# An edge convolution on a graph: which batches fetch their rows without gathers, and how far gathers and features are asked for ahead

## The chip, the cores and the metric

One core of a Trainium2 chip runs the kernel. The metric is the device time of one execution in microseconds, and the time given for the kernel is the median of its runs.

## The reference

Graph with N = 12500 nodes (160 features each) and 400000 edges sorted by destination. What is computed, with the weights' scalings left out:

```python
h = relu(layernorm(x))
y0 = h[:, :64] @ W_l1_0 * attr            # rows y = (y0, y1) of every node, 160 values
y1 = einsum('nuc,uv->nvc', h[:, 64:].reshape(n, 32, 3), W_l1_1) * attr
w  = silu(edge_attr_16 @ fc_W1) @ fc_W2   # 192 weights for each edge
ys0, ys1 = y0[src], y1[src]               # gather by edge
mid0 = concat([w_a * ys0 * e0, w_d * (ys1 . e1)])
mid1 = concat([(w_b * ys0) x e1, w_c * e0 * ys1])
z0, z1 = segment sums of mid0, mid1 over dst
out = x + C_S * (h0 @ W_sc0, h1 @ W_sc1) * attr + C_X * (z0 @ W_l2_0, z1 @ W_l2_1) * attr
```

Here e0 and e1 are the first and the other three columns of edge_attr_4.

## The kernel before, in words

**Node stage.** 98 tiles of 128 nodes, in steps of two (HN). x is loaded into acc, normalised, transposed, multiplied by wy and written as ys to a table y_d in HBM, from which the edge stage gathers rows. Beside it POOL already fetches rows of x (not y) for XB = 18 batches of edges into xr (`x_fetch`, L378): 72 indirect DMAs, each held back by a map (po, L485) six steps earlier. SP issues the loads of x, the stores of y_d (L497), the weights' loads (L296), the first features (L393), and `row_index` (L267): twelve DMAs that bring the source indices of the row batches into ri. At the end of the stage DVE scales ri to byte offsets (`row_place`, L271).

**Edge stage.** 3125 tiles of 128 edges, four tiles to a batch: NB = 782 batches. For batch b:
- rows of y come into a tile of yg (six buffers) by four indirect DMAs on POOL (`gather`, L603), one for each tile. They are asked for AHEAD batches before their use, two tiles at a time, and a dependency written by hand keeps the fetches behind the sums (L681) of the batch AHEAD places earlier.
- the features of the edges (xe, one block for eight batches) are asked for EARLY batches ahead on SP (`features`, L393).
- PE makes hidden values (L630; px) and weights (`weigh`, L651; pw), DVE multiplies them with the rows (`products`: own L665, sel L667, pr L561 and L565), PE sums by selection matrices into pz (`sums`, L681).
- sorted destinations let a group of four windows share one matrix: a window is 24, 12, 8, 6, 4 and at last 3 tiles, so a group is 24 down to 3 batches long (three from batch 624 on). At a group's end DVE transposes pz into za (L687, L688), PE applies wo (`linear`, L694) and places the result (`add`, L706), and DVE adds it to acc (L717).
- every 24 batches a block of indices and edge values is loaded on SP (`e4_load`, L401 to L405), related to its windows on DVE (`relate`), joined on ACT (`e4_join`), and its drel is stored by SP (L419).

Two kinds of batches need no gather on POOL:
- **x batches**, `x_batch(u)` for u < 18: every 16th batch from 19 on. Their rows of x lie in xr since the node stage. The mean and scale of each source node are looked up by PE with one-hot matrices (`hot`, `hot_turn` L776, `look_up` L788, `pick`), ACT centers the rows (`x_center`), PE transposes (`x_turn`, L803 and L804) and maps them (`x_map`, L816 and L817), and the scale goes into the edge values (`x_scale`, L823).
- **row batches**, `row_batch(i)`: 72 + 64i, twelve of them. SP fetches each of their 512 rows by a DMA of its own (`row_fetch`, L623), in chunks of 16 spread over the 64 batches from 64i on, into xr where an x batch has been, or, for the first, into a tile rg.

**Node pairs** (49; `skip_load` to `skip_add`) add the second product, h by ws, to acc: x is loaded again, centered, transposed (L741, L742), multiplied (L751, L752) and added (L760). They come every nine batches from batch 296 on, behind the last x batch.

The order of the instructions on each engine is the order of the program (a manual schedule); each engine waits where its next instruction's inputs or buffers aren't ready. SP runs through its part of the program ahead of the others.

Of the kernel before, what the change touches and what calls it, by code (L numbers as in the profile page):

```python
# [10 lines left out]
F32 = mybir.dt.float32  # L11
# [8 lines left out]
P = 128  # L20
M0 = 64
M1 = 32
D = M0 + 3 * M1
# [6 lines left out]
GT = 4  # L30
# [6 lines left out]
MW = BLK // WTS[-1]  # L37
GN = 8
HN = 2
AHEAD = 4  # L40
EARLY = 8
SB = 16
LATE = 8
XB = 18
SK = 9
RB = 64
RN = 16
LO = D - P
EPS = 1e-5
# [5 lines left out]
def kernel(  # L55
# [19 lines left out]
    nc = tc.nc  # L75
# [47 lines left out]
    GE = NG - LATE  # L123
# [20 lines left out]

    ygp = ctx.enter_context(tc.tile_pool(name="yg", bufs=6))
    ld = ctx.enter_context(tc.tile_pool(name="ld", bufs=2))
    evp = ctx.enter_context(tc.tile_pool(name="ev", bufs=2))
    rp = ctx.enter_context(tc.tile_pool(name="rel", bufs=2))
    RF = RB + 8
    NR = (NB - 1 - RF) // RB + 1  # L150
    RP = 4
    assert NR - 1 <= XB and RP * NR <= P
    ri = const.tile([RP * NR, P // RP * GT], I32, name="ri")
    rg = const.tile([P, GT, D], F32, name="rg")
    blocks, ev4, lows = {}, {}, {}

    before = ctx.enter_context(ExitStack())
# [105 lines left out]
    def row_index():  # L263
        t = row_batch(0) * GT
        for i in range(NR):
            t = row_batch(i) * GT
            nc.sync.dma_start(ri[RP * i:RP * (i + 1), :].rearrange("q (p k) -> q p k", k=GT),  # L267
                              src[:, t:t + GT].rearrange("(q p) k -> q p k", q=RP))

    def row_place():  # L270
        nc.vector.tensor_scalar(ri, ri, float(D * 4), None, ALU.mult)  # L271
# [86 lines left out]

    def x_batch(u):

        return SB * (u + 1) + 3

    def x_index(us):
        t = x_batch(0) * GT
        every = src[:, t:t + XB * SB * GT].rearrange("p (u r) -> p u r", r=SB * GT)[:, :, 0:GT]
        nc.sync.dma_start(xi[:, us, :], every[:, us, :])

    def x_split():

# [16 lines left out]
    def features(b):  # L386
        blk = b * GT // BT
        if blk not in blocks:

            xe = ld.tile([P, 512], F32, name="xe")  # L390
            v = e16[blk * P:(blk + 1) * P, :].rearrange("(s k f) (h c) -> k s (f h) c", s=4, k=2, h=2)
            for k in range(2):
                nc.sync.dma_start(xe[:, 256 * k:256 * (k + 1)], v[k])  # L393
            blocks[blk] = xe
# [30 lines left out]
    with (  # L425
# [81 lines left out]
        for i, (g, n) in enumerate(groups[:LEAD]):  # L507
            load_x(g, n)
            if i == 1:
                x_index(slice(2, XB))  # L510
                nc.sync.dma_start(a_sb, attr)
        last = len(steps) - 1
        more = list(groups[LEAD:])
# [1 line left out]
        for q in range(len(steps) + 7):  # L515
            if q <= last and steps[q][2] == 0 and more:
                load_x(*more.pop(0))
            for f in range(XB * GT * q // (last + 6), min(XB * GT * (q + 1) // (last + 6), XB * GT)):
                x_fetch(f, mapped.get(q - 6))
            if q == 8:  # L520
                e4_load(0)
            if q == 10:
                row_index()
            for load in loads[2 * q - 24:2 * q - 22] if q >= 12 else []:
                load()
            if q == 24:
                for b in range(min(EARLY, NB)):
                    features(b)
            if q == 16:
                rows_of_windows()  # L530
                lowest(0)
            if q == 18:
                pt = nd_ph.tile([MW, P], F32, name="ph")[:windows_in(0), :]
                turn_low(0, pt)
                most(0, pt)
            if q == 22:
                spread(0, nd_ph.tile([P, MW], F32, name="ph")[:, :windows_in(0)])
            for stage, lag in ((scales, 3), (leave, 7), (out_of_psum, 4), (roots, 2), (turn_rows, 3), (map_rows, 5),
                               (moments, 0), (center, 1)):
                if 0 <= q - lag <= last:  # L540
                    stage(q - lag)
            if q == 2:
                node_weights()
            if q == last + 3:
                nc.vector.tensor_scalar(nm, mv[:, :, 0], -1.0, None, ALU.mult)
                x_split()
                edge_weights()
                relate(rp, 0)
                row_place()
        assert 12 + len(loads) // 2 <= last and x_batch(XB) <= NB  # L550
    before.close()


# [14 lines left out]
    with (  # L568
# [43 lines left out]
        def row_fetch(i, n):  # L612

            b = row_batch(i)
            if n == 0:
                rows[b] = xr[:, i - 1, :, :] if i else rg
            q, o = divmod(n * RN, P // RP * GT)
            _, at_row = nc.values_load_multi_w_load_instructions(
                ri[RP * i + q:RP * i + q + 1, o:o + RN], engines=[mybir.EngineType.SP], min_val=0, max_val=(N - 1) * D * 4,
                skip_runtime_bounds_check_because="places of nodes, as the indices of the other fetches")  # L620
            for m, v in enumerate(at_row):
                e, k = divmod(n * RN + m, GT)
                nc.sync.dma_start(rows[b].bitcast(U8)[e:e + 1, k, :], y_b[ds(v, D * 4)].unsqueeze(0))  # L623
# [200 lines left out]

        NU = (NT + HN - 1) // HN
        skips = {4: skip_center, 5: skip_turn, 7: skip_map, 8: lambda u: skip_load(u + 1) if u + 1 < NU else None}
        SS, MAP = SB * XB + 8, 7
        xs_of = {x_batch(u) for u in range(XB)}
        rows_of = {row_batch(i) for i in range(NR)}
        assert not xs_of & rows_of and RF + RB * (NR - 1) < NB - 1  # L830
        chunks = [(i, n) for i in range(NR) for n in range(P * GT // RN)]

        K, KB = 3, BLK // GT
        waiting = []
# [7 lines left out]
        def extras(b):  # L842

            g = group_of[b]
            k = b - first_of[g]
            q, r = divmod(b, KB)
            u, v = divmod(b, SB)
            su, sv = divmod(b - SS, SK)
            if b % 2 == 0 and b + 4 < NB:
                s = (b + 4) // 2  # L850
                activate(s, hidden(s))
            if g and k == 0:
                linear(g - 1)
            if b == SS - 8:
                skip_load(0)
            skip = skips.get(sv) if 0 <= su < NU else None
            if skip and sv != MAP:
                skip(su)
            if r == KB - 11 and q + 1 < NQ:
                spread(q + 1, p_x.tile([P, MW], F32, name="px")[:, :windows_in(q + 1)])  # L860
            if u < XB:
                if v == 2:
                    hot_turn(u)
                elif v == 7:
                    x_center(u)
                elif v in (9, 10):
                    x_turn(u, HN * (v == 10))
                elif v == 11:
                    x_map(u, 0)
            if v == 1 and 0 < u <= XB:  # L870
                x_map(u - 1, HN)
            if g and k == 1:
                left(lambda: accumulate(g - 1))
                add(g - 1)
            if skip and sv == MAP:
                left(lambda: skip_add(su))
                skip(su)
            if u < XB and v in (3, 6):
                left(None)
                picked = look_up(u, HN * (v == 6))  # L880
                waiting[-1] = lambda: pick(u, HN * (v == 6), *picked)
            if r == KB - 6 and q + 2 == NQ:
                left(None)
                cnt = p_x.tile([1, 1], F32, name="px")
                any_far(cnt)
                waiting[-1] = lambda: far_flag(cnt)
            if r == KB - 13 and q + 1 < NQ:
                left(None)
                low_pt = p_x.tile([MW, P], F32, name="px")[:windows_in(q + 1), :]
                turn_low(q + 1, low_pt)  # L890
                waiting[-1] = lambda: most(q + 1, low_pt)
# [12 lines left out]
        for b in range(NB):  # L904
            g = group_of[b]
            k = b - first_of[g]
            if b + EARLY < NB:
                features(b + EARLY)
            q, r = divmod(b, KB)
            if r == 0:  # L910
                e4_load(q + 1)
            if r == KB - 4:
                e4_join(q + 1)
            u, v = divmod(b, SB)
            su, sv = divmod(b - SS, SK)
            if b + 2 < NB:
                weigh(b + 2)
            if b + 1 < NB:
                products(b + 1)
            while waiting and b + K < NB:  # L920
                waiting.pop(0)()
            if v == SB - 2 and u < XB:
                x_scale(u)
            if v == 11 and u + 1 < XB:
                hot(u + 1)
# [9 lines left out]
            for m, part in ((b + AHEAD - 1, slice(2, GT)), (b + AHEAD, slice(0, 2))):  # L935
                if AHEAD <= m < NB and m not in xs_of and m not in rows_of:
                    gather(m, part)
            while chunks and chunks[0][0] * RB + chunks[0][1] * RB * RN // (P * GT) <= b:
                row_fetch(*chunks.pop(0))
            while waiting and b + K >= NB:  # L940
                waiting.pop(0)()
            extras(b)
        while waiting:
            waiting.pop(0)()
        assert SS + NU * SK <= first_of[GE] + K and NQ > 1
        for h in ([NG - 2] if NG > 1 else []) + [NG - 1]:
            for k, stage in enumerate((linear, add, accumulate)):
                if h == NG - 1 or min(k, 1) > NB - 1 - first_of[NG - 1]:
# [159 lines left out]
```

## Time and profile before

| | |
|---|---|
| median of 3 runs | 3925.41 us (3924.81 to 3928.84) |
| the profiled execution | 3917.68 us |
| its span | 3915.5 us |
| PE busy | 3586.6 us (92%) |
| DVE busy | 2748.4 us (70%) |
| POOL busy | 2917.6 us (75%) |
| ACT busy | 623.6 us (16%) |
| moved by DMA | 329.82 MB, mean 84 GB/s |
| first gather of the edge stage starts | 100.48 us |
| last one starts | 3892.30 us |

How to read it: a row of the groups gives line, engine, operation, output and inputs with their shapes, a count, then busy time in us and the mean in ns of one, and behind the second bar the idle time of the engine just before these instructions with what ended it ("issue": nothing that the profile shows was waited for). A row of the waits gives who waited for whom: us in total, times, longest. A row of a timeline gives start, duration, and in brackets the idle time before. PEld is the weight load of PE. SPq is the queue of SP; its rows are DMA issues.

### The profile page before, as it was taken

How to read it: one execution, taken by the hardware profiler on the slowest of the kernel's cores; microseconds unless marked ns; L12 is line 12 of the kernel's file. 1: busy time of each engine (PE TensorE's matmuls, PEld its weight loads, DVE VectorE, ACT ScalarE, POOL GpSimd, SP SyncE). 2: the span in 40 equal slices, each digit the busy share in tenths (PEclk: the TensorE clock that was granted, in tenths of full speed). 3: DMA queues.
4: the chain of work that ended last, by engine and by line, in shares of the span. 5: the costliest groups of instructions: out<-in, count | busy, mean ns of one | idle time of the engine just before them, and what ended most of it. 6: DMA issues, size and time to landing. Idle time of an engine off the chain costs nothing.

```text
span 3915.5 us, 66013 instructions
## 1 busy us (share of the span) xinstructions
PE 3586.6 (92%) x17274; PEld 2321.5 (59%) x17274; DVE 2748.4 (70%) x6899; ACT 623.6 (16%) x1863; POOL 2917.6 (75%) x3085
## 2 busy tenths in 40 slices
PE   7898999999999999889999999989899999999988
PEld 7555555555656655555555565555566666666555
DVE  7566666666667666666677677777677777778776
ACT  6111111111111111111111111111111111111111
POOL 6777777777777777777777777777777777777775
PEclk8899999999999999999999999999999999999999
DMA  8333333323333232333333333333333333333324
GB/s 233 78 79 76 78 78 76 77 73 78 77 75 78 74 80 75 83 83 80 80 82 77 84 79 82 80 80 79 82 80 83 80 79 82 83 80 79 79 74 135
DMA packets 262773, 329.82 MB, mean 84 GB/s; under 512 B 78472, under 2 KB 213160, under 8 KB 262392
## 3 DMA queue, kind: packets, MB, share of 16 engines
q0 software_dynamic: 147696, 252.26, 26.2%
q1 hardware_dynamic: 114072, 73.01, 6.7%
q8 instruction: 140, 2.29, 0.2%
q14 instruction: 241, 1.97, 0.2%
q10 hardware_dynamic: 624, 0.27, 0.0%
HBM read 307.70 MB, written 17.61 MB: 83 GB/s over the span
## 4 chain that ended last, share of the span: by engine, by line
PE 42%; DMA 20%; DVE 18%; issue 11%; POOL 8%; DVEq 1%; SPq 0%; ACT 0%; POOLq 0%; ACTq 0%
PE pz L681 22%; DMA yg<-y_d,src_q 19%; POOL yg L603 8%; PE pw L651 8%; DVE pr L565 7%; PE px L630 5%; DVE pr L561 4%; PE px L694 3%; PE px L706 1%; DVE za L687 1%; DVE at L226 1%; DVE za L688 1%; DVE acc L717 1%; DVE own L665 0%; PE po L485 0%
## 5 line engine op out<-in xcount | busy, mean ns | idle before, releaser
L603 POOL DMA_INDIRECT yg<-y_d,src_q x3005 | 2847.2, 947 | 945.9 <-issue 658.2
L681 PE MATMUL pz<-pr,sel 128*128 128x320 f32 x6250 | 1965.7, 459 | 14.8 <-DVE za L688 14.7
L681 PEld LDWEIGHTS pz<-pr,sel 128*128 128x128 f32 x6250 | 1162.6, 196 | 597.9 <-issue 231.1
L561 DVE TENSOR_TENSOR pr<-pw,yg 128x512 f32<-128x512 f32 x752 | 517.9, 689 | 800.4 <-DMA yg<-y_d,src_q 799.2
L651 PE MATMUL pw<-w,hT 64*128 64x192 f32 x6250 | 737.4, 354 | 252.5 <-DVE pr L565 236.1
L651 PEld LDWEIGHTS pw<-w,hT 64*128 64x128 f32 x6250 | 506.1, 189 | 535.4 <-issue 396.8
L565 DVE TENSOR_TENSOR pr<-pw,yg 128x384 f32<-128x384 f32 x1504 | 760.7, 547 | 0.0
L667 DVE TENSOR_TENSOR sel<-own,pw 128x512 f32<-128x512 f32 x782 | 537.0, 687 | 27.0
L630 PE MATMUL px<-xe,w 32*128 32x512 f32 x782 | 437.3, 640 | 8.8 <-DVE acc L717 7.1
L635 ACT ACTIVATE hT<-px 128x512 f32<-128x512 f32 x391 | 233.4, 597 | 1297.1 <-PE px L630 1292.8
L556 ACT ACTIVATE pw<-ev 128x20 f32<-128x20 f32 x782 | 149.3, 191 | 1417.1 <-PE pw L651 1201.8
L687 DVE STREAM_TRANSPOSE za<-pz 128x160 f32<-128x160 f32 x598 | 203.8, 341 | 233.7 <-PE pz L681 232.8
L694 PEld LDWEIGHTS px<-wo,za 128*128 128x128 f32 x1500 | 211.5, 191 | 106.6 <-issue 68.0
L694 PE MATMUL px<-wo,za 128*128 128x160 f32 x1500 | 243.0, 309 | 8.8 <-DVE high L193 4.3
L630 PEld LDWEIGHTS px<-xe,w 32*128 32x128 f32 x782 | 114.2, 183 | 185.0 <-issue 173.3
L688 DVE STREAM_TRANSPOSE za<-pz 32x160 f32<-32x160 f32 x598 | 201.7, 337 | 20.4
L665 DVE TENSOR_TENSOR own<-iota,pw 128x128 f32<-128x128 f32 x782 | 198.4, 254 | 18.3 <-ACT pw L556 14.7
L706 PE MATMUL px<-os,place 128*128 128x160 f32 x600 | 112.0, 309 | 8.3 <-DVE place L698 3.6
L717 DVE SCALAR_TENSOR_TENSOR acc<-px,a_sb,acc 128x160 f32 x300 | 113.8, 379 | 7.5 <-PE px L706 1.5
L706 PEld LDWEIGHTS px<-os,place 128*128 128x128 f32 x600 | 90.7, 190 | 38.5 <-issue 19.7
L378 POOL DMA_INDIRECT xr<-in_x,xi x72 | 69.2, 962 | 29.2 <-PE po L485 13.7
L696 ACT ACTIVATE os<-px 128x160 f32<-128x160 f32 x150 | 45.6, 304 | 229.6 <-PE px L694 228.6
(131 smaller groups left out, 1380.1 us busy)
## 6 DMA issues: line engine op xcount, KB each, us to landing
xr<-y_d SPq DMA_DIRECT2D x5632, 0.6 KB
yg<-y_d,src_q POOLq DMA_INDIRECT x3005
xe<-in_e SPq DMA_DIRECT2D x196, 128.0 KB
rg<-y_d SPq DMA_DIRECT2D x512, 0.6 KB
xs<-in_x SPq DMA_DIRECT2D x48, 160.0 KB
acc<-in_x SPq DMA_DIRECT2D x11, 640.0 KB
y_d<-ys SPq DMA_DIRECT2D x11, 640.0 KB
out<-acc SPq DMA_DIRECT2D x11, 640.0 KB
```

Of the source, the lines that this page charges most:

```text
L561: nc.vector.tensor_mul(pr[:, :n, :].rearrange("p t (x u) -> p t x u", x=2)[:, :, :, 0:M0], wt[:, :n, 0:NW].rearrange("p t (x u) -> p t x u ...
L565: nc.vector.tensor_mul(pr[:, :n, D * x + M0:D * (x + 1)].rearrange("p t (c u) -> p t c u", c=3), wt[:, :n, 96 * x + M0:96 * (x + 1)].unsqu ...
L603: fetch = nc.gpsimd.indirect_dma_start(out=yg[:, slot(t), :], out_offset=None, in_=y_d, in_offset=bass.IndirectOffsetOnAxis(ap=ev4[t // BL ...
L630: nc.tensor.matmul(ph, w1[r, :], xe[r, :], start=True, stop=True)
L635: nc.scalar.activation(hT, ph, AF.Silu, scale=1.0 / math.sqrt(FC_IN))
L651: nc.tensor.matmul(pw[:, k, 0:NW], hT[r, o:o + P], w2[r, :], start=True, stop=True)
L667: nc.vector.tensor_tensor(sel, own[:, :n, :].unsqueeze(2).to_broadcast([P, n, 4, WN]), wt[:, :n, NW:NW + 4].unsqueeze(3).to_broadcast([P, ...
L681: mm = nc.tensor.matmul(pz[:, 0:PC], sel[:, slot(t), :, :], pr[:, slot(t), :], start=o == 0, stop=last)
L687: nc.vector.transpose(zT[g][:, :, at_w], pz[:, D:PC].rearrange("p (k u) -> p k u", k=ZK))
L688: nc.vector.transpose(zT[g][0:32, :, at_w], pz[0:32, 0:D].rearrange("p (k u) -> p k u", k=ZK))
L694: nc.tensor.matmul(po[:m, :], za[:, k, :m], wo[:, k, :], start=k == 0, stop=k == ZK - 1)
L706: nc.tensor.matmul(ps[:, h, :], place[:m, h, :], os[:m, :], start=True, stop=True)
```

## The change

- AHEAD from 4 to 6: gathers are asked for six batches ahead, behind the sums of the batch six earlier; yg keeps its six buffers.
- EARLY from 8 to 16, and xe gets a pool of its own with three buffers instead of two.
- x batches are PER = 43 apart (19, 62, ... 750) instead of 16 (19, 35, ... 291). Behind each one's work (the first 16 batches of a period) three node pairs follow in the same period, nine batches each; the last pair ends at batch 712.
- row batches are 92 + 61i, still twelve; their chunks begin at batch 24 + 61i. All twelve take a place in xr; rg is gone. `row_index` moves from the node stage to batch 0 of the edge stage, `row_place` to batch 2.
- the indices of the last x batch get a DMA of their own (`x_index_last`), since the strided view would reach beyond the array.
- `x_scale` runs 3 batches before its x batch instead of 5.

```diff
-AHEAD = 4
-EARLY = 8
+AHEAD = 6
+EARLY = 16
 SB = 16
+PER = 43
...
-RB = 64
+RB = 61
+RS = 24
...
+    fe = ctx.enter_context(tc.tile_pool(name="fe", bufs=3))
...
-    RF = RB + 8
+    RF = RS + RB + 7
...
-    rg = const.tile([P, GT, D], F32, name="rg")
...
 def x_batch(u):
-        return SB * (u + 1) + 3
+        return PER * u + SB + 3
...
+    def x_index_last():
+        t = x_batch(XB - 1) * GT
+        nc.sync.dma_start(xi[:, XB - 1, :], src[:, t:t + GT])
...
-            xe = ld.tile([P, 512], F32, name="xe")
+            xe = fe.tile([P, 512], F32, name="xe")
...
-                x_index(slice(2, XB))
+                x_index(slice(2, XB - 1))
+                x_index_last()
...
-            if q == 10:
-                row_index()
...
-                row_place()
...
-                rows[b] = xr[:, i - 1, :, :] if i else rg
+                rows[b] = xr[:, i, :, :]
...
-        SS, MAP = SB * XB + 8, 7
+        PAIRS, MAP = (PER - SB) // SK, 7
...
+        def skip_of(b):
+            u, v = divmod(b, PER)
+            if v < SB:
+                return -1, -1
+            return PAIRS * u + (v - SB) // SK, (v - SB) % SK
...
-            u, v = divmod(b, SB)
-            su, sv = divmod(b - SS, SK)
+            u, v = divmod(b, PER)
+            su, sv = skip_of(b)
...
-            if b == SS - 8:
+            if b == SB - 8:
                 skip_load(0)
...
-            if v == 1 and 0 < u <= XB:
-                x_map(u - 1, HN)
+            if v == SB + 1 and u < XB:
+                x_map(u, HN)
...
+            if b == 0:
+                row_index()
...
+            if b == 2:
+                row_place()
-            if v == SB - 2 and u < XB:
+            if v == SB and u < XB:
                 x_scale(u)
...
-            while chunks and chunks[0][0] * RB + chunks[0][1] * RB * RN // (P * GT) <= b:
+            while chunks and RS + chunks[0][0] * RB + chunks[0][1] * RB * RN // (P * GT) <= b:
                 row_fetch(*chunks.pop(0))
```

More of the change, by code (lines that the diff above doesn't have):

```diff
@@ L146 @@
     ld = ctx.enter_context(tc.tile_pool(name="ld", bufs=2))
+    fe = ctx.enter_context(tc.tile_pool(name="fe", bufs=3))
     evp = ctx.enter_context(tc.tile_pool(name="ev", bufs=2))
     rp = ctx.enter_context(tc.tile_pool(name="rel", bufs=2))
-    RF = RB + 8
+    RF = RS + RB + 7
     NR = (NB - 1 - RF) // RB + 1
     RP = 4
-    assert NR - 1 <= XB and RP * NR <= P
+    assert NR <= XB and RP * NR <= P and PER < RB
     ri = const.tile([RP * NR, P // RP * GT], I32, name="ri")
-    rg = const.tile([P, GT, D], F32, name="rg")
     blocks, ev4, lows = {}, {}, {}
@@ L359, in x_batch @@
     def x_batch(u):
-        return SB * (u + 1) + 3
+        return PER * u + SB + 3
     def x_index(us):
         t = x_batch(0) * GT
-        every = src[:, t:t + XB * SB * GT].rearrange("p (u r) -> p u r", r=SB * GT)[:, :, 0:GT]
+        every = src[:, t:t + (XB - 1) * PER * GT].rearrange("p (u r) -> p u r", r=PER * GT)[:, :, 0:GT]
         nc.sync.dma_start(xi[:, us, :], every[:, us, :])
+    def x_index_last():
+        t = x_batch(XB - 1) * GT
+        nc.sync.dma_start(xi[:, XB - 1, :], src[:, t:t + GT])
     def x_split():
@@ L548 @@
                 relate(rp, 0)
-                row_place()
-        assert 12 + len(loads) // 2 <= last and x_batch(XB) <= NB
+        assert 12 + len(loads) // 2 <= last and x_batch(XB - 1) < NB - 1
     before.close()
@@ L913 @@
                 e4_join(q + 1)
-            u, v = divmod(b, SB)
-            su, sv = divmod(b - SS, SK)
+            u, v = divmod(b, PER)
+            su, sv = skip_of(b)
             if b + 2 < NB:
@@ L944 @@
             waiting.pop(0)()
-        assert SS + NU * SK <= first_of[GE] + K and NQ > 1
+        assert max(b for b in range(NB) if 0 <= skip_of(b)[0] < NU) <= first_of[GE] + K and NQ > 1
         for h in ([NG - 2] if NG > 1 else []) + [NG - 1]:
```

## Prediction

> **What bounds the kernel now.** I read the page's busy times first, then the groups, then the waits, then POOL in order of time, then the windows.
>
> ```profile
> PE 3586.6 (92%) x17274; PEld 2321.5 (59%) x17274; DVE 2748.4 (70%) x6899; ACT 623.6 (16%) x1863; POOL 2917.6 (75%) x3085
> L603 POOL DMA_INDIRECT yg<-y_d,src_q x3005 | 2847.2, 947 | 945.9 <-issue 658.2
> ```
>
> By busy time PE is fullest. But the POOL group has 945.9 us of idle time in front of its gathers, and the waits tell what that is:
>
> ```profile
> DVE pr L561 <- DMA yg<-y_d,src_q: 799.2, 483, 5.7
> POOL yg L603 <- issue: 658.2, 2159, 0.4
> POOL yg L603 <- PE pz L681: 93.1, 248, 2.3
> ```
>
> Most of the idle time is 2159 gaps of 658.2 / 2159 = 0.305 us in which nothing was waited for. The gap belongs to the gather, as the timeline of POOL shows (start, duration, and the idle time before in brackets): one start every 1.25 us, whatever released it.
>
> ```profile
> 739.24 0.95 POOL L603 DMA_INDIRECT yg<-y_d,src_q  x1 [0.30 <-issue]
> 740.49 0.94 POOL L603 DMA_INDIRECT yg<-y_d,src_q  x1 [0.30 <-issue]
> 743.79 0.95 POOL L603 DMA_INDIRECT yg<-y_d,src_q  x1 [2.36 <-PE px L198]
> 745.05 0.95 POOL L603 DMA_INDIRECT yg<-y_d,src_q  x1 [0.30 <-issue]
> 746.81 0.94 POOL L603 DMA_INDIRECT yg<-y_d,src_q  x1 [0.82 <-PE pz L681]
> ...
> 3891.05 0.95 POOL L603 DMA_INDIRECT yg<-y_d,src_q  x1 [0.30 <-issue]
> 3892.30 0.95 POOL L603 DMA_INDIRECT yg<-y_d,src_q  x1 [0.30 <-PE pz L681]
> ```
>
> So a gather costs POOL 0.947 + 0.305 = 1.252 us, a batch of four 5.01 us, and all 3005 take 3762 us. The first starts at 100.48 (row below), the last ends at 3893.25: 3793 us. POOL sets the edge stage, and only 945.9 - 3005 x 0.305 = 29.4 us of that stretch are waits that could go. The windows say the same, and where the waits are (stretch, its length, then PE, PEld, DVE, ACT, POOL busy with counts, granted clock):
>
> ```profile
> 100.00:120.00 20.00, 11.69 (x53) 7.27 (x51) 8.48 (x17) 1.55 (x6) 15.12 (x17) 0.78 0.34 87
> 100.00:560.00 460.00, 407.85 (x1883) 253.45 (x1880) 286.56 (x643) 74.73 (x220) 346.88 (x367) 0.96 0.31 78
> 560.00:1020.00 460.00, 428.58 (x2001) 269.46 (x2000) 305.17 (x698) 78.58 (x229) 342.35 (x362) 0.97 0.31 76
> 1020.00:1480.00 460.00, 434.00 (x2077) 276.64 (x2076) 318.67 (x748) 80.20 (x235) 340.10 (x359) 0.98 0.31 76
> 2120.00:3120.00 1000.00, 924.02 (x4435) 597.99 (x4434) 729.12 (x1833) 135.49 (x420) 753.08 (x796) 0.97 0.32 80
> ```
>
> Gathers times 1.252: 460 of 460 us, 453 of 460, 449 of 460, 997 of 1000. The losses sit mainly where x batches are 16 apart: a batch that POOL needn't gather puts it 5 us ahead, it runs into the limit of four batches, and waits for the sums (743.79 and 746.81 are the gathers just behind row batch 136 with x batch 131 before it: 2.06 + 0.52 us over the usual gap).
>
> A rule weighed: the Trainium skill (Perfetto Trace Analysis, Identifying the Most-Contended Engine) says to improve the engine of highest occupancy, but not to judge TensorE by its matmul busy time. By PE's 92% nothing would come of fewer POOL waits, and the time would stay; by the page's measures (weight loads 59%, POOL 75%) POOL is the one, as the gaps above show.
>
> **The change part by part.**
>
> *Number of gathers.* 18 x batches and 12 row batches before and after (the last are 72 + 64i before, 92 + 61i after): still 3005 gathers, 3762 us. This floor doesn't move; the change can earn the 29.4 us and something in the node stage, no more.
>
> *Spread and lead of six.* Skipped batches come 30 in 782 evenly, one in 26, instead of 22 in the first 296 and 8 in the other 486. POOL's average need becomes 5.01 x 752 / 782 = 4.82 us a batch everywhere. PE must need less than that to catch up behind each skipped batch. Its need without extras, in the last part, where a group is only three batches long, from the chain at the end, which is all PE there (eight runs of sums, seven steps):
>
> ```profile
> 3859.69 2.35 PE pz L681 x8
> ...
> 3890.81 2.35 PE pz L681 x8
> ```
>
> 31.12 / 7 = 4.45 us a batch. The extras on PE (busy time of all their instructions):
>
> ```profile
> L752 PE MATMUL px<-ws,sT 128*128 128x96 f32 x196 | 40.5, 288 | 0.0
> L751 PE MATMUL px<-ws,sT 128*128 128x64 f32 x196 | 34.4, 257 | 1.5 <-DVE acc L717 1.5
> L788 PE MATMUL px<-look,sT 128*128 128x196 f32 x144 | 31.6, 342 | 0.0
> L817 PE MATMUL px<-wy,sT 128*128 128x96 f32 x144 | 29.8, 288 | 0.0
> L741 PE MATMUL px<-ident,sh 128*128 128x128 f32 x98 | 25.1, 283 | 4.1 <-ACT hT L635 4.1
> L816 PE MATMUL px<-wy,sT 128*128 128x64 f32 x144 | 24.9, 254 | 0.0
> L742 PE MATMUL px<-ident,sh 128*128 128x128 f32 x98 | 24.1, 273 | 0.0
> L803 PE MATMUL px<-ident,xr 128*128 128x128 f32 x72 | 18.8, 288 | 2.0 <-DVE acc L717 2.0
> L804 PE MATMUL px<-ident,xr 128*128 128x128 f32 x72 | 18.0, 277 | 0.0
> L776 PE MATMUL px<-ident,oh 128*128 128x128 f32 x72 | 11.8, 286 | 0.0
> ```
>
> An x batch: (11.8 + 31.6 + 18.8 + 18.0 + 24.9 + 29.8) / 18 = 7.5 us. A node pair: (25.1 + 24.1 + 34.4 + 40.5) / 49 = 2.5 us. After, 43 batches hold one x batch and three pairs: 15.1 / 43 = 0.35 a batch. So in the worst part PE needs 4.45 + 0.35 = 4.80 against POOL's 4.82: just enough. Earlier, with longer groups, it needs less. Locally, batches 624 to 712 hold the work of two x batches and 6.5 pairs: 88 x 4.45 + 31.4 = 423 us against 84 x 5.01 = 421 for POOL; then 712 to 782 (no pairs, one x batch): 319 against 68 x 5.01 = 341. PE falls behind by what the skipped batches give POOL, some 10 to 13 us, and makes it up before the end. Two batches more of lead are 2 x 4.8 = 9.6 us more room; the stalls that it must take in are about 2.6 us at the largest place shown. Twice (275 and 277, 578 and 580) two skipped batches are two apart: 5 us more, still inside. Remaining stalls: between 0 and 15 us; I take 3, near the 3.4 us that the stretch from 2120 lost with a lead of four. Edge stage: -26.4.
>
> The sixth buffer of yg is free in time: the gather waits for the sums of the batch six back, and the products that read the buffer come before these. So no wait is added that the lead itself doesn't bring.
>
> *Moved row indices (SP, DVE), third feature buffer.* SP in order of time:
>
> ```profile
> 3.25 3.40 SPq L511 DMA_DIRECT2D a_sb<-in_attr  x1
> ...
> 21.69 11.39 SPq L267 DMA_DIRECT2D ri<-in_src  x12
> 33.19 0.41 SPq L497 DMA_DIRECT2D y_d<-ys  x1
> ...
> 57.17 1.20 SPq L393 DMA_DIRECT2D xe<-in_e  x2
> ...
> 97.34 0.48 SPq L401 DMA_DIRECT2D raw<-in_e  x1
> ...
> 100.31 26.01 SPq L623 DMA_DIRECT2D rg<-y_d  x64
> ```
>
> The twelve issues held SP for 11.4 us in the node stage, with a store of y_d behind them. They go behind the last store, to about 98 to 110. There, behind them on SP, are the next block's indices (due at batch 18) and the row fetches, which now begin at batch 24: nothing due. The scaling of ri on DVE (0.28 us, row below) stands behind the products of batch 3, which need gathers that end at 120; ri should be there by 113. Cost 0. In the node stage come two issues of xe (1.2 us) and one more of xi (under the 3.4 us of the nearest row). What the node stage gains goes through POOL, which does 72 fetches there:
>
> ```profile
> POOL xr L378 <- PE po L485: 13.7, 24, 2.2
> 71.81 0.94 POOL L378 DMA_INDIRECT xr<-in_x,xi  x1 [2.22 <-PE po L485]
> 75.94 0.94 POOL L378 DMA_INDIRECT xr<-in_x,xi  x1 [0.68 <-PE po L485]
> 100.48 0.94 POOL L603 DMA_INDIRECT yg<-y_d,src_q  x1 [0.30 <-issue]
> L271 DVE TENSOR_SCALAR ri<-ri 48x128 int32<-48x128 int32 x1 | 0.3, 280 | 0.0
> ```
>
> 13.7 - 24 x 0.305 = 6.4 us of true waits at most; if SP was not the cause, 0, or +2 for the added issues. I take the two late ones, 1.92 + 0.38: -2.3. Row fetches: 26.01 / 64 = 0.406 us an issue, 208 us for 512, in 61 x 4.82 = 294 us instead of 64 x 4.85 = 310; the last is issued by batch 83 of 92, 39 us ahead: 0. Features 16 ahead: no wait for xe is among the large ones, 0 (a late one is bounded by SP's 1.2 us).
>
> *End.* From the last gather to the span's end, 22.3 us. The last skipped batch is 763 instead of 776, so there are 18 batches to drain what PE is behind; 0 to +5, I take +1.
>
> **Sum:** -26.4 - 2.3 + 1 = -27.7 us. The profiled execution took 3917.68 (span 3915.5), so 3890; it lies 7.7 us under the median of 3925.41, so the median should come to 3898.
>
> **The rivals.**
> *PE becomes the bound* in the last 158 batches. For it: 4.80 against 4.82 is no margin, and hand-overs cost PE something. Against: the chain's 4.45 has its hand-overs in it. At 4.90 it gives back 158 x 0.08 = 13 us: 3911.
> *The lead isn't what stalls POOL* (the sums are late for another reason, at every skipped batch as now): 29.4 us stay and only the node stage gains: 3923. Against: the stalls stand right behind skipped batches.
> *The clock turns it round (slower).* The first 300 batches lose x work: PE's need falls from 4.7 x 407.85 / 460 = 4.2 (100 to 560: 367 gathers are 92 batches, with six skipped ones 98 in 460 us, 4.7 each) to 4.2 - 7.5 / 16 + 0.35 = 4.1 of 4.82 us. PE then pauses more, and with PE busy 58% the clock was 0.78 (100 to 120), at 89% it was 0.96. Below 4.1 x 0.96 / 4.82 = 0.82 PE would decide; at 0.78 it needs 5.05, 0.23 x 300 = 69 us more: 3967. Against: at 85% busy the line between those two rows gives 0.94. The Trainium skill (TensorE: Matmul & The Clock Gate, The HAM clock gate) has the clock halved after an idle window of about 3.4 us; no single wait need reach that here, since DVE's waits for yg average 799.2 / 483 = 1.7 us, though the longest is 5.7. By that rule the forecast stands.
>
> **How the numbers follow.** The forecast has 0.74, PE as the bound 0.16, the lead without effect 0.05, the clock 0.05. About 0.2% (8 us) is what a measurement here can tell from no change. The low end is all waits gone: 3925.4 - 29.4 - 6.4 = 3889. The high end takes in half of the PE case, 3911; outside are the last two cases and the other half of PE's, 0.18. Faster is the first case and nearly all of the second, 0.88; same 0.07; slower 0.05.
>
> **What would show it.** Right: POOL's gathers still 3005 of 947 ns, their idle time down from 946 to about 920, POOL's waits for sums near the usual gap, the last gather ending near 3865, the issues of ri near 100, the first row fetch not before batch 16's relation to its windows, about 185. Wrong: stalls of several us behind 641, 664, 702 and 707; PE without pauses from batch 624 to the end; a longer gather; a clock under 0.85 before 1480; DVE waiting for rows in xr.

## The result, and the profile after

The changed kernel takes 3894.65 us in the median of four runs (3892.13 to 3897.29) against 3925.11 us before: ratio 0.9922, 95% interval 0.9905 to 0.994, that is about 30 us less. The profiled execution took 3892.68 us with a span of 3890.6.

From the page of the changed kernel (busy times, the gathers' group; line 607 was 603) and from its waits (total, times, longest):

```profile
PE 3588.1 (92%) x17274; PEld 2323.1 (60%) x17274; DVE 2750.5 (71%) x6899; ACT 622.3 (16%) x1863; POOL 2924.2 (75%) x3085
L607 POOL DMA_INDIRECT yg<-y_d,src_q x3005 | 2854.3, 950 | 916.7 <-issue 658.6
```

```profile
DVE pr L565 <- DMA yg<-y_d,src_q: 713.0, 417, 5.4
POOL yg L607 <- issue: 658.6, 2159, 0.3
...
POOL yg L607 <- PE pz L685: 70.5, 231, 0.3
```

The idle time before the gathers is 916.7 us, and 3005 x 0.305 is 916.5: nothing but the gap that belongs to each gather. In the row of waits for pz the longest is 0.3 us, where it was 2.3. POOL doesn't stop once between its first gather and its last one:

```profile
97.49 0.95 POOL L607 DMA_INDIRECT yg<-y_d,src_q  x1 [0.31 <-DMA ri<-in_src]
98.74 0.94 POOL L607 DMA_INDIRECT yg<-y_d,src_q  x1 [0.30 <-issue]
...
3867.27 0.95 POOL L607 DMA_INDIRECT yg<-y_d,src_q  x1 [0.30 <-issue]
```

So the span splits into three: the first gather starts 3.0 us earlier (97.49 for 100.48); between first start and last end 3770.7 us for 3792.8; then 22.4 for 22.3. Of the middle, 29.9 us of waits went (all gaps of over 0.35 us, summed over 0.305), and 7.8 us came back because a gather took 949.9 ns in this execution instead of 947.5 (2.4 ns) and its gap was a little longer. -3.0 - 29.9 + 7.8 + 0.1 = -25.0, which is the difference of the spans, 24.9.

The windows of the changed kernel (stretch, length, PE, PEld, DVE, ACT, POOL busy, clock, DMA share) show a POOL that is equally full everywhere, and PE close behind it late:

```profile
100.00:560.00 460.00, 400.35 (x1774) 246.08 (x1774) 273.59 (x628) 62.02 (x186) 348.23 (x367) 0.93 0.32 79
1020.00:1480.00 460.00, 419.27 (x1977) 265.39 (x1977) 309.38 (x736) 67.08 (x203) 348.23 (x367) 0.97 0.32 80
3130.00:3570.00 440.00, 429.47 (x2146) 284.31 (x2142) 358.12 (x914) 68.97 (x211) 332.92 (x352) 1.00 0.31 79
```

SP after, in order of time:

```profile
22.66 2.29 SPq L503 DMA_DIRECT2D y_d<-ys  x1
...
50.33 2.87 SPq L399 DMA_DIRECT2D xe<-in_e  x4
...
94.96 9.09 SPq L269 DMA_DIRECT2D ri<-in_src  x12
104.09 0.47 SPq L407 DMA_DIRECT2D raw<-in_e  x1
...
216.72 5.38 SPq L627 DMA_DIRECT2D xr<-y_d  x16
```

The store of y_d that stood behind the index loads until 33.19 now goes at 22.66, and the row fetches begin at 216.7.

### The profile page after: what moved, and what is told of

Its sections match the earlier page's. It is cut to its first block, busy times and chain, and to the rows that moved or that the text cites. A ratio compares the mean times of both kernels' runs of the same rounds, so it can differ in the third digit from the quotient of the medians.

```text
span 3890.6 us, 66031 instructions
## 1 busy us (share of the span) xinstructions
PE 3588.1 (92%) x17274; PEld 2323.1 (60%) x17274; DVE 2750.5 (71%) x6899; ACT 622.3 (16%) x1863; POOL 2924.2 (75%) x3085
## 4 chain that ended last, share of the span: by engine, by line
PE 52%; DMA 16%; DVE 14%; issue 10%; POOL 6%; SPq 1%; DVEq 1%; ACT 0%; POOLq 0%; ACTq 0%
PE pz L685 28%; DMA yg<-y_d,src_q 15%; PE pw L655 10%; POOL yg L607 6%; PE px L634 6%; DVE pr L569 5%; PE px L698 4%; DVE pr L565 4%; PE px L710 1%; DVE at L228 1%; DVE za L691 1%; DVE za L692 1%; SPq L627 1%; DVE acc L721 0%; PE po L491 0%
## 5 line engine op out<-in xcount | busy, mean ns | idle before, releaser
L607 POOL DMA_INDIRECT yg<-y_d,src_q x3005 | 2854.3, 950 | 916.7 <-issue 658.6
```

What stands on the lines that cost most here:

```text
L607: fetch = nc.gpsimd.indirect_dma_start(out=yg[:, slot(t), :], out_offset=None, in_=y_d, in_offset=bass.IndirectOffsetOnAxis(ap=ev4[t // BL ...
```

## The experiments

Each set of runs has its own time of the kernel before, taken on the same chip, since chips differ: 3917.64 us in the first set (lead_only, spread_only, index_early, no_pairs) and 3917.39 in the last (rows14, rows6). Two sets in between ran on chips on which the kernel before takes 4714.89 and 4711.5 us; they are told apart. A ratio is always to the kernel before of the same set.

**The lead alone (lead_only).**

```diff
 # the kernel before
-AHEAD = 4
+AHEAD = 6
```

> The kernel before with the lead of six alone (x batches 16 apart, row batches 64 apart, row indices in the node stage). Theory A, the room of the lead is what takes in the skipped batches: POOL's 29 us of waits for sums vanish or nearly so although the x batches still come in a crowd, because PE's need (about 4.4 us a batch) is under POOL's 4.61 of the first 296 batches; 3925 - 26 = about 3899, with the idle time before the gathers at 917 to 922 us. Theory B, the crowding is what costs: POOL gains 5 us at each x batch faster than PE makes it up, reaches the limit of six as it reached that of four, and only the first stalls go: idle time 930 to 940, time about 3912.

Measured: 3887.19 us, ratio 0.9924 (0.991 to 0.9937), the same ratio as the whole change within the intervals. Its gathers, and the first of them:

```profile
L603 POOL DMA_INDIRECT yg<-y_d,src_q x3005 | 2847.1, 947 | 915.9 <-issue 651.3
```

```profile
99.19 0.95 POOL L603 DMA_INDIRECT yg<-y_d,src_q  x1 [0.30 <-issue]
```

No wait is left (the longest gap before a gather is 0.32 us), with the x batches still 16 apart. That is theory A.

**The spacing without the lead (spread_only).**

```diff
 # the changed kernel
-AHEAD = 6
+AHEAD = 4
```

> The changed kernel with the lead back at four; the spacing of 43 and 61, the later features and the moved indices stay. Theory A (room of the lead): each of the 30 skipped batches still runs into the limit of four, about 1 us each, more in batches 624 to 712 where PE has no margin: 20 to 35 us of waits, so 3917 to 3925 with the 3 us of the node stage kept. Theory B (crowding): the waits are mostly gone by the spacing alone, under 10 us left, 3898 to 3905.

Measured: 3920.2 us, ratio 1.0007 (0.9998 to 1.0016). The group, and POOL's timeline behind row batch 763:

```profile
L607 POOL DMA_INDIRECT yg<-y_d,src_q x3005 | 2846.7, 947 | 950.7 <-issue 670.3
```

```profile
3804.78 0.95 POOL L607 DMA_INDIRECT yg<-y_d,src_q  x1 [0.30 <-issue]
3809.50 0.95 POOL L607 DMA_INDIRECT yg<-y_d,src_q  x1 [3.77 <-PE pz L685]
3810.75 0.95 POOL L607 DMA_INDIRECT yg<-y_d,src_q  x1 [0.30 <-issue]
...
3814.91 0.94 POOL L607 DMA_INDIRECT yg<-y_d,src_q  x1 [0.72 <-PE pz L685]
...
3820.84 0.94 POOL L607 DMA_INDIRECT yg<-y_d,src_q  x1 [1.23 <-PE pz L685]
```

The waits are 34.8 us, behind 21 of the 30 skipped batches, 0.1 to 4.8 us each; before they were 29.9 us behind 20. Spread apart, a skipped batch still puts POOL a whole batch ahead, and a lead of four didn't hold that in 21 of 30 cases. Theory A again: crowding isn't the cause, the room is, and the spacing earns nothing that the lead doesn't earn alone.

The profile before says so too, when its waits are summed by skipped batch: the 22 that stand close together, up to batch 291, cost 19.8 us, which is 0.9 us each; the eight behind them, 64 apart, cost 10.1 us, which is 1.3 us each. The largest sum, 3.6 us, is behind row batch 520, far from any x batch:

```profile
2604.34 0.94 POOL L603 DMA_INDIRECT yg<-y_d,src_q  x1 [2.35 <-PE pz L681]
...
2608.40 0.94 POOL L603 DMA_INDIRECT yg<-y_d,src_q  x1 [1.87 <-PE pz L681]
```

**Would a lead of five do?** Both runs with five fell on chips where POOL isn't the bound (below), but the traces from the faster chips tell. A gather that is held starts 0.27 us after the sums that it waits for have ended (272 to 274 ns, in the profile before and in that of the spacing alone). In the trace of the lead alone, the sums that a lead of five would name have ended at least 0.84 us before every gather's start, in that of the changed kernel at least 0.57 us. So a lead of five would have held no gather in either; a lead of four would have held 109 and 141. This is worked out from traces at six, and no run shows the time. In the traces of rows14 and rows6 five would have held one gather each, by under 0.3 us.

**Row indices back in the node stage (index_early).**

```diff
 # the changed kernel
+            if q == 10:
+                row_index()
...
+                row_place()
...
-            if b == 0:
-                row_index()
...
-            if b == 2:
-                row_place()
```

> The changed kernel with the twelve loads of row indices and their scaling back in the node stage. If their 11.4 us on SP are what held the node stage up, the first gather starts at 100 to 101 again instead of 97.5, the fetches of x rows wait 2.5 us more, and the time is 3 us above the changed kernel's 3894.7. Rival: the earlier start came from something else (run to run), then 97.5 and no difference.

Measured: 3892.44 us, ratio 0.9936 (0.9922 to 0.995). SP and POOL in its node stage:

```profile
22.66 11.47 SPq L269 DMA_DIRECT2D ri<-in_src  x12
34.25 0.41 SPq L503 DMA_DIRECT2D y_d<-ys  x1
```

```profile
76.91 0.94 POOL L384 DMA_INDIRECT xr<-in_x,xi  x1 [6.24 <-PE po L491]
...
105.36 0.95 POOL L610 DMA_INDIRECT yg<-y_d,src_q  x1 [0.30 <-issue]
```

The first gather starts at 105.4, later than expected (100 to 101) and later than before (100.5). POOL waits once for 6.24 us in the node stage, where the longest wait there was 2.22 before. Against the kernel before, this node stage has two more issues of xe and one more of xi on SP; that these are the reason isn't shown. In the kernel without pairs (next), which ran beside it with the changed node stage, the first gather starts at 96.98; the spans differ by 7.7 us, about as much as the starts (8.4). The move is worth about that, given the earlier features. On that chip every run of index_early (3890.75 to 3894.54 us) is longer than every run without pairs (3885.67 to 3887.90), which also has less work; the changed kernel itself didn't run there, and its ratio's interval overlaps that of index_early, so the size rests on the profiles.

**Without the node pairs (no_pairs).**

```diff
 # the changed kernel
-            if b == SB - 8:
-                skip_load(0)
-            skip = skips.get(sv) if 0 <= su < NU else None
+            skip = None
```

> The changed kernel without the 49 node pairs: their loads, transposes, maps and additions to acc are left out, 124 us of PE and some 60 us of DVE. Theory A, POOL sets the time everywhere: the gathers keep their pace of 1.255 us, the last ends near 3868 as before, and the time stays within 3 us of 3894.7. Theory B, PE is the bound in the later part after the change (4.80 against 4.82 us a batch): the time falls by 5 to 20 us, through an earlier last gather or a shorter end.

This kernel leaves out the second product, h by ws, which the node pairs would add to acc. Measured: 3886.13 us, ratio 0.9922 (0.9907 to 0.9937), the changed kernel's ratio to the last digit. Its first and last gathers:

```profile
96.98 0.94 POOL L607 DMA_INDIRECT yg<-y_d,src_q  x1 [0.30 <-issue]
...
3859.10 0.95 POOL L607 DMA_INDIRECT yg<-y_d,src_q  x1 [0.30 <-issue]
```

The pairs' matmuls are gone, 125 us by their own rows, and the gathers take 3763 us as with the lead alone. PE, nearly full in 3130 to 3570, isn't the bound. PE's busy time fell by 67 us only (3588.1 to 3521.1), and by 6 in that window (429.47 to 423.70), so a busy share near 100% doesn't mean here that PE has no time left.

**More and fewer row batches, on the lead alone (rows14, rows6).**

```diff
 # the kernel before with AHEAD = 6
-RB = 64
+RB = 52     # rows14: 14 row batches
...
-RB = 64
+RB = 128    # rows6: 6 row batches
```

> The lead of six on the kernel before, row batches 52 apart: 14 instead of 12, so 2997 gathers and 1024 row fetches more on SP. On a chip where the kernel before takes about 3920 us: theory A, POOL alone sets the time, 8 x 1.252 = 10 us under the lead alone, ratio 0.9898 (the work of SP, 198 us more for each row batch, fits into its waits for drel and for indices, about 740 us). Rival, SP falls behind: ratio 0.992 or more. On a chip where it takes 4712: 1.10 as before.

> The lead of six on the kernel before, row batches 128 apart: six instead of twelve, so 3029 gathers and 3072 row fetches fewer on SP. On a chip where the kernel before takes about 3920 us: POOL sets the time, 24 x 1.252 = 30 us above the lead alone, ratio 1.000. On a chip where it takes 4712: if SP's row fetches (0.67 us each there) set the time, it falls to about 4100 or below (ratio 0.87); rival, all engines are slow there alike and the row fetches aren't the bound: ratio 0.98 to 1.01.

Measured: rows14 3879.57 us, ratio 0.9904 (0.9889 to 0.9919); rows6 3909.6 us, ratio 0.9981 (0.9972 to 0.999). The gathers of the one and the other, and the waits of SP in rows14:

```profile
L603 POOL DMA_INDIRECT yg<-y_d,src_q x2997 | 2840.4, 948 | 913.6 <-issue 664.3
```

```profile
L603 POOL DMA_INDIRECT yg<-y_d,src_q x3029 | 2869.1, 947 | 923.0 <-issue 657.0
```

```profile
SPq L403 <- DMA yg<-y_d,src_q: 141.9, 51, 6.8
SPq L419 <- DVE za L687: 127.0, 16, 36.3
```

The idle time is 0.305 us for each gather in both, so POOL sets the time in both, and it moves with the number of gathers: 2840.4 + 913.6 = 3754 us with 2997 gathers, 3763 with the 3005 of the lead alone, and 3792 with 3029. rows14 is the fastest kernel here, 8 us under the lead alone (10 expected: its first gather starts 3 us later, behind 14 index loads in the node stage); the two ran on different chips and their ratios' intervals overlap, so the order rests on the gathers. SP had room: its waits for drel behind za fell from 318.2 us (lead alone, row below) to 127.0. rows6 is 22 us above the lead alone and not 30: behind its last gather only 17.8 us follow, instead of 22 to 24. Why its end is shorter isn't shown.

```profile
SPq L419 <- DVE za L687: 318.2, 18, 21.2
```

**On the two slower chips (after_again, lead5, more_rows, early8, lead5_b, after_b).** after_again and after_b are the changed kernel, lead5 and lead5_b the kernel before with AHEAD = 5, early8 the changed kernel with EARLY = 8, more_rows the kernel of rows14.

> The changed kernel once more, beside the others. Its first profile had gathers of 949 ns in the median where all other profiles had 946 (7 us over 3005 gathers). Theory A, that belonged to that execution or chip: 946 here, and a time some 5 us nearer to the lead alone (ratio 0.992 to 0.993). Theory B, the layout of the buffers or the lead makes a gather longer: 949 again.

> The kernel before with a lead of five instead of four. One batch of room is 4.8 us; the largest sum of stalls behind one skipped batch is 3.6 us before. Theory A, room takes in the stalls up to its size: all or nearly all of the 29.9 us vanish with five already (under 3 us left), time as with six (ratio 0.992 to 0.994). Theory B, the lead works in proportion (half the room, half the gain): about 15 us left, ratio 0.996.

> The kernel before with the lead of six and row batches 52 apart instead of 64: 14 of them, so eight gathers fewer on POOL and 1024 row fetches more on SP. Theory A, POOL is the only bound: 8 x 1.252 = 10 us less than the lead alone, ratio 0.9898. Rival, SP: 512 issues take 208 us of the 52 x 4.8 = 250 us between two row batches, and with its waits for drel (16 us in 24 batches) SP falls behind; then DVE waits for rows in xr and the time is as with the lead alone or above (ratio 0.992 or more).

> The changed kernel with features asked for 8 batches ahead instead of 16; the three buffers stay. No wait for xe was among the large ones before, so nothing should change in the edge stage; in the node stage two issues of xe fewer on SP: 0 to 3 us off the first gather's start. Rival, that the later features had hidden a late block: waits of PE or DVE for xe appear, some us more.

> The kernel before with a lead of five, again, where the row fetches hold SP about 0.4 us each and not 0.67 as in the last set (there SP set the time, and no lead could help). Theory A, room takes in the stalls up to its size: under 3 us of POOL's waits are left of 29.9, ratio 0.992 to 0.994 as with six. Theory B, in proportion: about 15 us left, ratio 0.996. If a row fetch takes 0.67 us again: ratio 1.00.

> The changed kernel, beside lead five. With gathers of 946 ns: first gather at 97, 3763 us of gathers without a wait, 22 to 24 us behind: span 3883 to 3885, ratio 0.9915 to 0.993. If a row fetch takes 0.67 us again, SP sets the time and the ratio is 1.008, because the row fetches start 24 batches later and have a shorter stretch.

Measured against 4714.89 us before: after_again 1.0079 (1.0049 to 1.011), lead5 1.001 (0.9994 to 1.0026), more_rows 1.1004 (1.0975 to 1.1033), early8 1.0091 (1.0063 to 1.012). Against 4711.5: lead5_b 1.0006 (0.999 to 1.0021), after_b 1.01 (1.0074 to 1.0126). POOL in lead5_b, and SP there:

```profile
L603 POOL DMA_INDIRECT yg<-y_d,src_q x3005 | 2844.9, 947 | 1720.5 <-issue 729.8
```

```profile
2000.09 6.33 SPq L623 DMA_DIRECT2D xr<-y_d  x14
...
2008.29 21.22 SPq L623 DMA_DIRECT2D xr<-y_d  x26
```

A gather takes the same 947 ns, but POOL waits 1720.5 - 916.5 = 804 us for others. Where POOL isn't the bound, more lead earned nothing, and the changed kernel is 1% slower than the kernel before. The granted clock of PE is also lower there: 0.90 in the mean of the profiled executions, 0.86 in more_rows, for 0.97 on the other chips.

What bounds the kernel before and lead5 there isn't settled. The expectations put it down to SP's row fetches. For that speaks that the fetches come further apart: 0.65 us in the mean from the start of one to the start of the next in lead5_b, and 0.61 in more_rows, for 0.39 with the lead alone. Against it speaks that hardly anything waits for what SP loads: in lead5_b no engine waits more than 10.3 us in all for xe, xr or xs by the profile. (For 359 us of DVE's waits the profile doesn't know what ended them.) PE has 344 us of idle time there for which the profile names no reason, and none such with the lead alone; ACT has more as well.

In more_rows SP is too late. Its 1024 row fetches more go with 474 us more (0.46 us each), and PE now waits for the features that SP loads between them:

```profile
PE px L630 <- DMA xe<-in_e: 522.6, 50, 19.3
```

Two smaller costs show in the same way. In the changed kernel DVE waits 56.6 us (after_again) and 68.9 us (after_b) for xs, the x of the node pairs, which SP loads too; that this is its 1% isn't shown. With EARLY = 8 PE waits 40.4 us for xe, with 16 only 4.6 (after_again). The earlier features thus took away a wait on that chip, as the rival in the expectation of early8 said, though the intervals of the two ratios overlap. What they do on a faster chip stays open; lead_only gets along without them.

after_again settles one thing: its gathers took 946 ns in the median, after_b's 949, lead5's 949 and lead5_b's 946, so the 2 to 3 ns belong to an execution and not to the change.

## Why the prediction was right

*POOL's pace as the floor, 29.4 us above it.* Right: 3005 gathers, 0.305 us before each, and no wait left, where 3 us of waits were taken to remain. The Trainium skill (Perfetto Trace Analysis, Identifying the Most-Contended Engine) takes occupancy as a fair measure for GPSIMD. Here 75% was a full POOL, because the gap before each gather isn't counted as busy.

*Spread and lead.* The sum was right, its ascription was not: the prediction put both into one term and made the spacing its first argument. The lead alone gives all of it, the spacing alone nothing (34.8 us of waits). So the number came out although one of the two reasons given for it was wrong. What the prediction said of the cause, a skipped batch puts POOL 5 us ahead and into the limit, is what both runs show; that it is so at any distance was not drawn from it. Its reading that the losses sit mainly where x batches are 16 apart holds for their sum (19.8 of 29.9 us), not for one skipped batch (0.9 us there, 1.3 elsewhere). The largest stall behind one skipped batch was 3.6 us, not 2.6.

*PE in the later part, 4.80 against 4.82.* PE kept up: 429.47 of 440 us busy and no wait of POOL, and leaving out the pairs changes nothing. The rival of PE as the bound fell. The reckoning was on the safe side. In the trace of the changed kernel the sums of a batch end 6.4 to 15.9 us after its last gather; across a skipped batch this lag grows by 2.4 to 4.9 us (once by 7.1), and then it shrinks again. From batch 624 to 710 it goes from 12.4 to 15.4 us, so PE falls behind by 3 us there and not by 10 to 13.

*Node stage, -2.3.* Measured -3.0 in the start of the first gather, and the store of y_d goes at 22.66 for 33.19, as the prediction had it. The size is uncertain: lead_only, with the node stage of the kernel before, starts at 99.19 and not 100.48. The three profiles on faster chips with the moved indices start at 97.0 to 97.5, so between 1.7 and 3.5 us are gained. In the old node stage the start also follows the number of index loads: 98.4 with six (rows6), 102.3 with fourteen (rows14). The scaling of ri cost nothing, as said: it starts at 120.5, and DVE waits there for none of the index loads.

*End, +1.* Measured +0.1.

*The clock.* 0.93 in the window 100 to 560, with PE busy 87%, where the line between two rows gave 0.94 at 85%. The rival of the clock fell on this chip.

*Not in the sum:* the 7.8 us of slightly longer gathers in the profiled execution. A longer gather was among the signs of being wrong, but it belongs to the execution. Because of it the spans differ by 24.9 us where 27.7 was forecast; the medians of the runs, 30.5 us apart, lie on the other side of the forecast. That the forecast stands between the two is partly luck: the waits and the node stage gave more than was taken, the gathers took some back.

## What to carry to other kernels

Where one engine serves at a fixed pace and some items skip it, its buffers must take in a whole item that is skipped, plus what the consumer is behind; size the lead by that, before rearranging the items. Here one batch more than the old lead of four would have been enough by the traces. Divide the idle time by the count first: a constant gap is part of the price of an instruction, and only what lies above it can be won. Such a gain hangs on that engine being the bound, so it can vanish on a chip where another one is.

## What the runs showed of the hardware

A gather by POOL takes 947 to 950 ns in the mean and has a gap of 0.305 us before it that isn't counted as busy, in every profile of this case. A gather that is held starts 0.27 us after the end of the sums that release it. The kernel before took 3917 to 3925 us in three sets of runs, and 4712 and 4715 us on two other chips. On those a gather and its gap were unchanged, while SP's fetches of single rows came 0.61 to 0.65 us apart in the mean instead of 0.39, and the granted clock of PE was 0.90 instead of 0.97 (0.86 in more_rows).
